# Values by tokens through DRAM, and base weights scaled by a norm, in a two-layer attention and FFN kernel

## The chip, the cores and the metric

The kernel runs on one core of one Trainium2 chip. The metric is the device time of one execution in microseconds (us), the median over runs. The core has TensorE for matmuls, VectorE and ScalarE, which read the matmul results in PSUM and work elementwise, GpSimd, which works elementwise on SBUF, and SyncE, whose queue issues every DMA of this kernel.

## What is computed

The input `x` and the context `ctx` are 32 batches of 128 x 1024, in f32. Two layers run one after the other on each batch; `LN` is a layer norm without weights.

```python
# layer 0, attention: autocorrelation of LN(x) with ctx, per head of 128 columns
corr = ifft(fft(q) * conj(fft(k))).real           # along the 128 rows
w, idx = top_k(corr, 9); w = softmax(w)
out += w[i] * v[min(idx[i] + pos, 127)]           # for the 9 best, v = ctx
x = x + out
# layer 0, FFN: base linear layer plus LoRA experts, the best 2 of 8
x = x + LN(x) @ W_base.T + b_base + lora(LN(x))
# layer 1, attention: 128 channels (rows), 1024 positions t (columns), 8 heads of 16 channels
q = Wq @ LN(x) + bq; k = Wk @ ctx + bk; v = Wv @ ctx + bv
k, v = pad(k, 8 left, 7 right, zeros), pad(v, same)
attn = softmax over the 16 positions t-8 .. t+7 of (q_t . k_j) / 4
x = x + Wo @ (attn . v) + bo
# layer 1, FFN: LoRA experts, the best 2 of 4
out = x + lora(LN(x))
```

## The kernel before

**Precision.** Most matrix products are made of f16 pieces: an operand is scaled, its high part is rounded to f16, and its low part is the remainder in f16. A product is then three f16 matmuls (high x high, high x low, low x high), accumulated in PSUM; the helper `three` and the table `THREE` stand for this. `split(hi, lo, src, eng)` makes the pieces: a ScalarE copy to the high part and a subtraction on VectorE or GpSimd (`G`). Some smaller products are done in f32 or in the matmul type f32r.

**Tiles.** `U()` is a 128 x 512 f32 buffer (tile u, 43 of them), `B()` a PSUM bank (p, all 8), `M()` 128 x 128 (m), `s()` small columns (s and t), and class `d` two buffers of 128 x 1024 f32. Any of them is given to an operation when the operation is placed, and comes free when its last user is done. Fixed tiles are, among others, `wsp` (the split base weights with the LoRA matrix and the router), `k16` (the split keys with 8 columns of zero padding on each side), `vpad` (the same for the values, high and low part side by side in one 4-byte word), `qbd` and `vbd` (block-diagonal stationary operands of the window attention).

**Stages of a batch**, by the names that the code gives to `P.stage`: `load` (ctx as `c`, x; ctx is scaled by its largest column maxima to the f16 pieces `c16`), `spec` (DFT of ctx; four copies inside SBUF move half of the partitions of each half batch), `corr`, `top` (the nine largest, on VectorE, and their softmax), `wt`, `inv`, then `ffn0`, `gate` and `base` for the first FFN, `kv`, `q`, `S` (scores), `PV`, `wo` for the second attention, and `ffn1`.

**The values.** In stage `kv`, `attention` computes V by channels: for each half of 512 positions, `three(p, wv16, c16[g])` gives 128 channels x 512 positions; ScalarE evicts it with scale and bias, and `split` writes both pieces to `vpad`. VectorE turns 32 x 32 blocks of `vpad`, seen as 4-byte words, through overlapping windows of 32 positions with a step of 16, into two tiles of class `d`, so that positions lie on partitions. For each half g and each group of 32 channels, an SP DMA then copies `d` to `vbd` in pieces of 128 bytes. `vbd` is one fixed tile: the loads of one half wait until PV of the half before is done. In stage PV, for each of 64 blocks of 16 positions, three matmuls of 32 columns take a 128 x 128 slice of `vbd` as weights and the split, transposed attention weights as the moving operand.

**The weights.** `prep_ffn` (stage `ws`) loads the base weights in 16 chunks of 128 x 512. VectorE takes the largest absolute value of each chunk per partition into `mx`, and likewise for the LoRA matrices; these are reduced over partitions with a transpose, and the results give the factors `wsc` (to the f16 range) and `wus` (back). Then the chunks are scaled and split into `wsp`.

**Order.** No engine's order is that of the code. A `Planner` records every operation with an estimated duration and then simulates the five engine queues in time; what it places on an engine, in which order, is emitted as written. Its priority for an operation is a period times the batch number, less the estimated length of the chain that follows, less a bias for the stage. `CFG` holds these numbers for two phases of time, with how many batches may be open at once (`win`: 5) and how many free buffers are kept back. After some batches the order repeats with a period.

All operations are recorded through one helper, so the profile gives nearly all of them the same line (L363); they are told apart by tile names and shapes.

Of the kernel before, what the change touches and what calls it, by code (L numbers as in the profile page):

```python
# [22 lines left out]
S = 128  # L23
# [5 lines left out]
CFG = {'nu': 43, 'nd': 2, 'en': 'G', 'cl': 'G', 'xl': 'G', 'sm': 'V', 'sw': 'A', 'wg': 'VG', 'q0': 'G', 'ns': 28, 'nt': 48, 'plan': {'phases': [{'at': 0.0, 'T': 19.88, 'margin': 178, 'win': 5, 'su': 60, 'sp': 3, 'ru': 1, 'rp': 0, 'bias': {'kv': -5.1, 'load': 10.0, 'S': -6.7, 'gate': 38.6, 'ffn1': 7.4, 'q': 0.4, 'top': 1.3, 'PV': -5.6, 'inv': 3.4, 'wt': 4.5, 'spec': 5.4, 'wo': 41.4, 'ws': -9.4, 'base': -1.7, 'ffn0': 90.1, 'corr': 5.4, 'setup': -12.6}}, {'at': 1459.1, 'T': 30.14, 'margin': 69, 'win': 6, 'su': 57, 'sp': 1, 'ru': 2, 'rp': 1, 'bias': {'kv': -32.9, 'load': -45.0, 'S': 18.4, 'gate': 125.0, 'ffn1': -67.8, 'q': 29.1, 'top': -23.6, 'PV': -37.2, 'inv': 57.1, 'wt': -20.7, 'spec': -56.0, 'wo': -29.3, 'ws': -71.2, 'base': -21.0, 'ffn0': 60.9, 'corr': -125.0, 'setup': 2.0}}], 'slack': [1.013, 0, 0]}}  # L29
# [11 lines left out]
class _View:  # L41
# [27 lines left out]
    def windows(self, n, step, width):  # L69
        return self._step("__getitem__", (slice(None), slice(0, 1)))._wrap(n, step, width)  # L70

    def _wrap(self, n, step, width):
        f = lambda ap: bass.AP(ap.tensor, ap.offset, [list(ap.ap[0]), [step, n], [1, width]])
        return _View(self.tile, f(self.proto), self.path + ((f, None, None),))

# [5 lines left out]

    def region(self):

        ap = self.proto
        size = mybir.dt.size(ap.dtype)
        dims = [list(d) for d in ap.ap]
        row = dims[0][0]
        p0, f0 = divmod(ap.offset, row)
        last = f0 + sum(s * (n - 1) for s, n in dims[1:])
        return p0, p0 + dims[0][1], f0 * size, (last + 1) * size  # L90


class _Tile:
    def __init__(self, cls, slot=None, const=False):
        self.cls, self.slot, self.const = cls, slot, const
        self.log, self.users = [], {}
# [9 lines left out]
class Planner:  # L106
# [72 lines left out]
    def _cost(self, op, method, v, kw):  # L179
# [21 lines left out]
        if eng == "Activation":  # L201
            op.dur += (n + (61 if src.proto.space == PSUM else 112)) / 1.2 + 94 * (nsc + ("accum_out" in v))
            if src.region()[0] != out.region()[0]:
                op.dur += 127.0
            elif out.proto.ap[-1][0] > 1:
                op.dur += 0.2 * n
        elif eng == "DVE":
            n = max(n, size(src))
            two = method in ("tensor_copy", "tensor_scalar", "memset") and not psum and n > 64
            op.dur += 6 * n / 0.96 + 67 if method == "reciprocal" else (n * (0.5 if two else 1.0) + 64 + 59 * nsc) / 0.96  # L210
            op.dur += 70.0 * ("accum_out" in v) + {"match_replace": 67.0, "transpose": 25.0}.get(method, 0.0)
        elif eng == "Pool":
            small = mybir.dt.size(out.proto.dtype) == 2
            if method == "memset":
                op.dur += 40.0 + (0.85 if small else 0.2) * n
            else:
                rate = (2.8 if small else 1.2) if method == "tensor_scalar" else 1.88 if small else 2.1
                if any(x.proto.ap[-1][0] == 0 for x in v.values()) and n > 128:
                    rate = 1.67
                op.dur += 530.0 if kw.get("op") == ALU.pow else 150.0 + rate * n  # L220
        else:
            run = out.proto.ap[-1][1] * mybir.dt.size(out.proto.dtype)
            dram = any(x.tile is None for x in v.values())
            op.dur += (3200.0 if dram else 2900.0 if run > 128 else 3500.0) + out.shape[0] * n * mybir.dt.size(out.proto.dtype) / 360.0

            op.cold = 450.0 if dram else 720.0 if run > 128 else 840.0

# [6 lines left out]
    def plan(self, phases, slack):  # L234
# [45 lines left out]
        while events:  # L280
            now = events[0][0]
            if phases and now >= phases[0][0]:
                period, window, margin, scarce, reserve, bias = phases.pop(0)[1]
                prio = lambda o: (period * max(o.batch, 0) - o.tail - bias.get(o.stage, 0.0), o.index)
                ready = {e: sorted((prio(o), o) for _, o in l) for e, l in ready.items()}
# [80 lines left out]
def plan_args(c):  # L366
    us = lambda v: v * 1e3
    scarce = lambda f: {"u": f["su"], "p": f["sp"], "d": 9, "m": 3, "r": 9, "s": 9, "t": 9}
# [6 lines left out]
def mk_kernel(ctx: ExitStack, tc: tile.TileContext, T: dict, out: bass.AP):  # L375
# [5 lines left out]
    pp = ctx.enter_context(tc.tile_pool(name="psum", bufs=1, space=PSUM))  # L381

    def slot(name, shape, dt=F32):
# [4 lines left out]
        "d": [slot(f"d{i}", [128, D]) for i in range(CFG["nd"])],  # L388
# [30 lines left out]

    def load(name, shape=None, dt=F32):  # L420
# [19 lines left out]
    G.memset(mhalf, -0.5)  # L440

# [20 lines left out]
    vpad = keep("vpad", [128, D + 16, 2], F16, 0.0)  # L462
# [21 lines left out]
    PE.matmul(pb[:, 0:3], lhsT=blk1, rhs=bsum, start=True, stop=True)  # L484
    bqs, sq, bqsc, uq = (const(n, [128, 1]) for n in ("bqs", "sq", "bqsc", "uq"))
# [6 lines left out]
    V.tensor_scalar(kvs[:, 1:2], rows[:, 2:3], C_SC / W_SC, None, op0=ALU.mult)  # L492
    V.tensor_scalar(kvb[:, 0:1], pb[:, 2:3], TINY, 1.0 / W_SC, op0=ALU.add, op1=ALU.mult)
    V.tensor_scalar(kvb[:, 1:2], absb[:, 2:3], TINY, 1.0 / W_SC, op0=ALU.add, op1=ALU.mult)
    V.tensor_scalar(rsx, rows[:, 1:3], 1.0 / W_SC, None, op0=ALU.mult)
# [25 lines left out]
    def prep_ffn():  # L521
# [10 lines left out]
        for k in range(16):  # L532
            t = U()
            SP.dma_start(out=t, in_=T["wbT"][k // 2 * 128 : (k // 2 + 1) * 128, k % 2 * HALF : (k % 2 + 1) * HALF])
            absmax(mx[:, k : k + 1], t)
            wb.append(t)
        for i in range(4):
# [7 lines left out]
        for i, (lo, hi) in enumerate(((0, 16), (16, 20), (20, 24), (24, 26), (26, 28))):  # L545
# [274 lines left out]
    def attention(b, x, c16, m1, sums):  # L820
        P.stage = "kv"

        bd, skv, bsc, esc, usc, eh = s(2), s(2), s(2), s(2), s(1), s(2)
# [3 lines left out]
        G.tensor_tensor(bsc, bkv_raw, skv, op=ALU.mult)  # L827
# [5 lines left out]
        for g in range(2):  # L833
            sl = slice(8 + g * HALF, 8 + (g + 1) * HALF)
            for i, (w, hi, lo) in enumerate(((wk16, k16[:, 0, sl], k16[:, 1, sl]), (wv16, vpad[:, sl, 0], vpad[:, sl, 1]))):
                t, p = U(), B()
                three(p, w, c16[g])
                A.activation(t, p, AF.Identity, bias=bsc[:, i : i + 1], scale=esc[:, i : i + 1])
                split(hi, lo, t, G)

        words = vpad.bitcast(U32).rearrange("p n i -> p (n i)")
        v16 = []
        for g in range(2):
            t = P.tile("d")
            tv = t.bitcast(U32).rearrange("p (b c) -> p b c", c=32)
            for h in range(2):
                V.transpose(tv[:, h * 16 : (h + 1) * 16], words[:, (2 * g + h) * 256 :].windows(16, 16, 32))
            v16.append(h16(t).rearrange("p (b c i) -> p b c i", b=32, i=2))
# [18 lines left out]
        for g in range(2):  # L867
# [4 lines left out]
            for hp in range(4):  # L872
                hs = slice(32 * hp, 32 * hp + 32)
                SP.dma_start(out=vbd[hs, :, hs], in_=v16[g][hs])
# [39 lines left out]
            V.scalar_tensor_tensor(x[g], p, bo, x[g], op0=ALU.add, op1=ALU.add, accum_out=sums[:, g : g + 1])  # L914
# [90 lines left out]
def _arrays(i):  # L1005
# [11 lines left out]
        "woT": a["L1_xattn_Wo"].T,  # L1017
# [22 lines left out]
```

## Time and profile before

| | |
|---|---|
| median of 3 runs | 1600.08 us (1599.47 to 1602.74) |
| profiled execution | 1600.9 us, its span 1599.1 us, mean granted TensorE clock 0.974 |
| TensorE busy | 1520.9 us, 95% of the span, 19144 matmuls |
| VectorE, ScalarE, GpSimd busy | 1468.7 us (92%), 1417.8 us (89%), 1346.0 us (84%) |
| DMA | 145.72 MB, queue busy 47.8% of 16 engines |
| first and last V matmul | 117.8 us, 1544.3 us |

A profile line of a group reads: engine, operation, output tile, input tiles, shapes, count, then busy time in us and the mean duration of one in ns, and the idle time just before these instructions with what ended it. Tile names stand without their numbers: u is any of the 128 x 512 buffers. A timeline line begins with start and length in us, and several equal instructions in a row are one line with a count. A line of the chain of waits begins with start and length in us. The granted clock is that of TensorE, as a share of full speed. The end of a matmul is modelled, so the pace of matmuls is read from starts.

### The profile page before, as it was taken

Reading aid. Unit: us, or ns where it says so; the run is one execution under the profiler, and the core shown is the slowest. Engines: PE = TensorE matmul, PEld = TensorE weight load, DVE = VectorE, ACT = ScalarE, POOL = GpSimd, SP = SyncE. Lnnn points to the kernel's source line nnn. Section 1 sums busy time; section 2 is a strip of 40 time slices with the busy share of each in tenths; the row PEclk is TensorE's granted clock in tenths of the full one; section 3 lists DMA queues with packets and bytes.
Section 4 is the critical chain, followed back from the end, with each engine's and each line's share of the span. In section 5 each row is a group of like instructions: output and inputs, shape, how many; then the busy total and the mean of one; then the engine's idle time right before and its main releaser. Section 6 shows DMA issues by size and latency. Waiting matters only on the chain.

```text
span 1599.1 us, 51794 instructions
## 1 busy us (share of the span) xinstructions
PE 1520.9 (95%) x19144; PEld 1001.9 (63%) x19144; DVE 1468.7 (92%) x5042; ACT 1417.8 (89%) x2833; POOL 1346.0 (84%) x1506
## 2 busy tenths in 40 slices
PE   2599999999999999999999999999999999999985
PEld 1256666666666666666666666666666666666654
DVE  6778999999999999999999999999999999999875
ACT  4998999999999999999999999999999999999753
POOL 5789878998888899888889988888998888899742
PEclk7789999999999999999999999999999999999996
DMA  8214544554454555445455544545455454554352
GB/s 267 81 56 57 98 63 91 102 105 91 91 91 70 94 102 106 91 91 92 69 96 101 105 91 92 93 68 96 100 105 92 90 95 68 95 100 78 41 70 58
DMA packets 854620, 145.72 MB, mean 91 GB/s; under 512 B 808224, under 2 KB 810528, under 8 KB 854368
## 3 DMA queue, kind: packets, MB, share of 16 engines
q1 hardware_dynamic: 854368, 142.41, 47.8%
q8 instruction: 152, 2.49, 0.7%
q14 instruction: 100, 0.82, 0.2%
HBM read 41.80 MB, written 16.78 MB: 37 GB/s over the span
## 4 chain that ended last, share of the span: by engine, by line
PE 90%; DVE 3%; ACT 2%; issue 1%; DMA 1%; POOL 1%; SPq 1%; POOLq 0%; DVEq 0%; ACTq 0%
PE p L363 90%; ACT u L363 2%; DVE u L363 1%; POOL u L363 1%; SPq L363 1%; DVE wsp L363 0%; DVE t L363 0%; DMA cf<-in_cf 0%; DVE s L363 0%; DMA u<-u 0%; DVE wmx L363 0%; DMA vbd<-d 0%; DVE mm L363 0%; DMA qbd<-u 0%; ACT k L363 0%
## 5 line engine op out<-in xcount | busy, mean ns | idle before, releaser
L363 POOL TENSOR_TENSOR u<-u,u 128x512 f32<-128x512 f32 (+1 forms) x640 | 774.9, 1233 | 94.4 <-ACT u L363 86.8
L363 PE MATMUL p<-wsp,u 128*128 128x512 f16 (+1 forms) x2304 | 409.9, 328 | 1.8 <-DVE r L363 0.9
L363 ACT ACTIVATE u<-p 64x512 f32<-64x512 f32 (+1 forms) x576 | 331.9, 591 | 52.0 <-PE p L363 43.7
L363 ACT ACTIVATE u<-u,t 128x512 f32<-128x512 f32 (+1 forms) x448 | 320.7, 723 | 62.3 <-DVE t L363 46.6
L363 DVE SCALAR_TENSOR_TENSOR u<-p,u 128x512 f32<-128x512 f32 (+1 forms) x448 | 289.2, 681 | 54.4 <-PE p L363 27.3
L363 PEld LDWEIGHTS <-u 128*128 128x128 f16 x3072 | 218.2, 98 | 167.0 <-issue 4.2
L363 ACT ACTIVATE u<-p,t 64x512 f32<-64x512 f32 (+3 forms) x448 | 265.7, 619 | 21.1 <-PE p L363 15.0
L363 PE MATMUL p<-u,ch 128*128 128x512 f16 x960 | 239.1, 385 | 1.9 <-DVE u L363 1.9
L363 PEld LDWEIGHTS <-qbd 128*128 128x128 f16 x6144 | 172.0, 96 | 27.1 <-issue 11.1
L363 PE MATMUL p<-k,qbd 128*128 128x32 f16 x6144 | 174.6, 176 | 1.6 <-issue 1.1
L363 PEld LDWEIGHTS <-ch 128*128 128x128 f16 x960 | 95.3, 102 | 120.7 <-issue 27.3
L363 PEld LDWEIGHTS <-vbd 128*128 128x128 f16 x6144 | 164.0, 97 | 8.5 <-issue 1.4
L363 PE MATMUL p<-u,vbd 128*128 128x32 f16 x6144 | 164.4, 176 | 0.7 <-POOL u L363 0.7
L363 ACT ACTIVATE u<-u,t,t 128x512 f32<-128x512 f32 x192 | 144.0, 820 | 5.2 <-POOL t L363 5.2
L363 POOL TENSOR_TENSOR t<-t,mhalf 128x1 f32<-128x1 f32 x128 | 71.5, 558 | 79.4 <-DVE t L363 79.0
L363 POOL TENSOR_TENSOR u<-u,s 128x512 f32<-128x512 f32 x128 | 134.2, 1050 | 0.7
L363 PE MATMUL p<-u,cf 128*128 128x512 f32 x256 | 125.2, 611 | 10.0 <-POOL u L363 10.0
L363 DVE SCALAR_TENSOR_TENSOR u<-p,t,u 128x512 f16<-128x512 f32 (+1 forms) x192 | 106.0, 567 | 16.9 <-ACT u L363 8.7
L363 ACT ACTIVATE u<-u 128x512 f16<-128x512 f32 x194 | 117.3, 623 | 3.4 <-DVE u L363 3.3
L363 PE MATMUL p<-ident,u 128*128 128x128 f32 x768 | 104.4, 279 | 10.6 <-ACT u L363 10.5
L363 PEld LDWEIGHTS p<-ident,u 128*128 128x128 f32 x768 | 90.8, 144 | 22.5 <-ACT u L363 13.4
L363 ACT ACTIVATE u<-p,t,t 128x512 f32<-128x512 f32 x128 | 94.0, 775 | 0.3 <-PE p L363 0.3
(155 smaller groups left out, 2863.8 us busy)
## 6 DMA issues: line engine op xcount, KB each, us to landing
vbd<-d SPq DMA_DIRECT2D x256, 128.0 KB
u<-u SPq DMA_DIRECT2D x192, 128.0 KB
u<-in_ctx SPq DMA_DIRECT2D x64, 256.0 KB
u<-in_x SPq DMA_DIRECT2D x64, 256.0 KB
qbd<-u SPq DMA_DIRECT2D x512, 32.0 KB
out<-u SPq DMA_DIRECT2D x64, 256.0 KB
u<-u SPq DMA_DIRECT2D x64, 126.0 KB
u<-in_wbT SPq DMA_DIRECT2D x16, 256.0 KB
```

The source lines that it names most:

```text
L363: fn(*[f(a) for a in args], **{k: f(a) for k, a in kw.items()})
```

## The change

**Values.** V is computed by tokens: for each block of 128 positions, the three pieces of the context are the weights (128 x 128) and `wv16` is the moving operand with 128 columns, so 12 matmuls of 128 columns fill one bank for each half. ScalarE evicts the high part to every second f16 place of a buffer, VectorE makes the low part from PSUM beside it, and an SP DMA writes the 512 positions (512 bytes each) to a DRAM tile, `vd[b % 2]`. The four `vbd` loads of each half read this DRAM tile in windows, in pieces of 128 bytes. `vpad`, class `d` and the VectorE transposes are gone.

As channels lie along the free dimension now, one scale serves all of them: the largest row sum and the largest bias over channels, made in setup (`gm`). The bias of V is not added to V: it goes through Wo into the output bias (`bo2`), and the padding rows hold the negative of the bias (`nbv`) instead of zero. Each batch writes these 2 x 8 padding rows by two small SP DMAs, after two ScalarE copies and a GpSimd subtraction on 16 partitions.

**Weights.** Instead of the 16 maxima on VectorE, ScalarE squares each chunk and sums the squares along the row (half a row of 1024); VectorE takes the largest of the 16 sums and GpSimd its square root.

**Plan.** `nu` goes from 43 to 49 u buffers, `nd` goes away. The numbers of `CFG` are others: the first phase has `win` 6, the second begins at 1494.3 in the planner's time instead of 1459.1, and each phase has biases for a stage on one engine too (`o.stage + "/" + o.eng`); estimated durations are stretched by 1.036 instead of 1.013, and DMAs get 0.27 us more. A DRAM tile counts as one region for dependencies.

```diff
-                prio = lambda o: (period * max(o.batch, 0) - o.tail - bias.get(o.stage, 0.0), o.index)
+                prio = lambda o: (period * max(o.batch, 0) - o.tail - bias.get(o.stage, 0.0) - bias.get(o.stage + "/" + o.eng, 0.0), o.index)
...
+    vd = []
+    for i in range(2):
+        vd.append(P.fixed(dp.tile([D + 16, 256], F16, tag=f"vd{i}", name=f"vd{i}")))
+        vd[i].tile.whole = True
...
+    mv, mx2, mb2, gm = const("mv", [128, 2]), s(1), M(), const("gm", [128, 2])
+    V.tensor_copy(mv[:, 0:1], rows[:, 2:3])
+    V.tensor_copy(mv[:, 1:2], absb[:, 2:3])
+    PE.transpose(pb[0:2, 128:256], mv, ident)
+    V.tensor_reduce(mx2[0:2], pb[0:2, 128:256], axis=AX.X, op=ALU.max)
+    V.tensor_copy(mb2[0:2], _bcast(mx2[0:2, 0], 128))
+    PE.matmul(pb[:, 256:258], lhsT=mb2[0:2], rhs=ident[0:2, 0:2], start=True, stop=True)
+    V.tensor_copy(gm, pb[:, 256:258])
+    bvr, nbv, bo2 = U(), const("nbv", [16, 128]), const("bo2", [128, 1])
+    SP.dma_start(out=bvr[0:16, 0:128], in_=T["bvr"].broadcast_to([16, 128]))
+    V.tensor_scalar(nbv, bvr[0:16, 0:128], -1.0, None, op0=ALU.mult)
+    PE.matmul(pb[:, 264:265], lhsT=woT, rhs=bkv_raw[:, 1:2], start=True, stop=True)
+    V.tensor_scalar(bo2, pb[:, 264:265], bo, None, op0=ALU.add)
...
-            absmax(mx[:, k : k + 1], t)
+            A.activation(U(), t, AF.Square, accum_out=mx[:, k : k + 1])
             wb.append(t)
+        V.tensor_reduce(mx[:, 30:31], mx[:, 0:16], axis=AX.X, op=ALU.max)
+        V.tensor_scalar(mx[:, 31:32], mx[:, 30:31], TINY, None, op0=ALU.add)
+        G.tensor_tensor(mx[:, 0:1], mx[:, 31:32], half, op=ALU.pow)
...
-            for i, (w, hi, lo) in enumerate(((wk16, k16[:, 0, sl], k16[:, 1, sl]), (wv16, vpad[:, sl, 0], vpad[:, sl, 1]))):
-                t, p = U(), B()
-                three(p, w, c16[g])
-                A.activation(t, p, AF.Identity, bias=bsc[:, i : i + 1], scale=esc[:, i : i + 1])
-                split(hi, lo, t, G)
-        words = vpad.bitcast(U32).rearrange("p n i -> p (n i)")
-        v16 = []
-        for g in range(2):
-            t = P.tile("d")
-            tv = t.bitcast(U32).rearrange("p (b c) -> p b c", c=32)
-            for h in range(2):
-                V.transpose(tv[:, h * 16 : (h + 1) * 16], words[:, (2 * g + h) * 256 :].windows(16, 16, 32))
-            v16.append(h16(t).rearrange("p (b c i) -> p b c i", b=32, i=2))
+            t, p = U(), B()
+            three(p, wk16, c16[g])
+            A.activation(t, p, AF.Identity, bias=bsc, scale=esc[:, 0:1])
+            split(k16[:, 0, sl], k16[:, 1, sl], t, G)
+        vb = vd[b % 2]
+        t, u = M(), M()
+        pads = h16(u).rearrange("p (n r) -> p n r", r=2)
+        A.activation(t[0:16], nbv, AF.Copy, scale=skv[0:16, 1:2])
+        A.activation(pads[0:16, :, 0], nbv, AF.Copy, scale=skv[0:16, 1:2])
+        G.tensor_tensor(pads[0:16, :, 1], t[0:16], pads[0:16, :, 0], op=ALU.subtract)
+        for i in range(2):
+            SP.dma_start(out=vb[i * (D + 8) : i * (D + 8) + 8], in_=h16(u)[8 * i : 8 * i + 8])
+        for g in range(2):
+            t, p = h16(U()), B()
+            with P.group():
+                for n in range(4):
+                    for i, (m, r) in enumerate(THREE):
+                        PE.matmul(p[:, n * 128 : (n + 1) * 128], lhsT=c16[g][:, m, n * 128 : (n + 1) * 128],
+                                  rhs=wv16[:, r], start=i == 0, stop=i == 2)
+            v = t.rearrange("p (n r) -> p n r", r=2)
+            A.activation(v[:, :, 0], p, AF.Copy, scale=esc[:, 1:2])
+            V.scalar_tensor_tensor(v[:, :, 1], p, esc[:, 1:2], v[:, :, 0], op0=ALU.mult, op1=ALU.subtract)
+            SP.dma_start(out=vb[8 + g * HALF : 8 + (g + 1) * HALF].rearrange("(n p) e -> p n e", p=128),
+                         in_=t.rearrange("p (n e) -> p n e", n=4))
...
-                SP.dma_start(out=vbd[hs, :, hs], in_=v16[g][hs])
+                SP.dma_start(out=vbd[hs, :, hs].rearrange("p b n r -> p b (n r)"),
+                             in_=vb.grid(g * HALF * 256 + 64 * hp, ((256, 32), (16 * 256, 32), (1, 64))))
...
-            V.scalar_tensor_tensor(x[g], p, bo, x[g], op0=ALU.add, op1=ALU.add, accum_out=sums[:, g : g + 1])
+            V.scalar_tensor_tensor(x[g], p, bo2, x[g], op0=ALU.add, op1=ALU.add, accum_out=sums[:, g : g + 1])
```

## The prediction, made before the changed kernel had run

> **What bounds the kernel now.** I read the page's engine table and slices first, then the granted windows, the chain of waits in order of time, the groups by shape, and last the timeline of TensorE and ScalarE.
>
> ```profile
> PE 1520.9 (95%) x19144; PEld 1001.9 (63%) x19144; DVE 1468.7 (92%) x5042; ACT 1417.8 (89%) x2833; POOL 1346.0 (84%) x1506
> PE   2599999999999999999999999999999999999985
> ```
>
> TensorE is the busiest engine, and its idle time sits in the first two slices and the last two. The windows cut the span there (columns: busy us of each engine, granted clock, DMA share, GB/s):
>
> ```profile
> 0.00:100.00 100.00, 49.73 (x189) 28.28 (x190) 75.81 (x279) 71.87 (x139) 67.83 (x81) 0.74 0.48 148
> 100.00:217.00 117.00, 113.48 (x1282) 72.24 (x1281) 102.10 (x343) 106.08 (x208) 106.31 (x113) 1.00 0.44 76
> 217.00:1508.00 1291.00, 1290.97 (x16566) 853.55 (x16566) 1231.70 (x4266) 1195.45 (x2404) 1136.19 (x1271) 1.00 0.50 90
> 1508.00:1600.00 92.00, 66.69 (x1111) 47.86 (x1109) 59.09 (x155) 44.39 (x87) 35.62 (x44) 0.82 0.40 64
> ```
>
> From 217 to 1508 us TensorE never stops, at full clock; 50.3 us of its idle lie before 100, 3.5 between 100 and 217, 24.4 behind 1508 (the span ends at 1599.1). The chain of waits says the same, and what ends last outside the long stretch:
>
> ```profile
> 22.27 6.07 DMA u<-u
> 30.35 2.96 DVE wmx L363 x5
> 33.38 2.01 DVE wmx L363 x10
> 36.93 0.79 DVE mm L363 x4
> ...
> 217.03 1290.31 PE p L363 x16561
> 1508.05 2.73 DMA vbd<-d
> ```
>
> A second such wait of 2.71 us stands at 1554.5. So three stages have three limits: a start led by VectorE (chain 28 to 57 us) and then by all elementwise engines, a long stretch that only TensorE's own work can move, and a serial tail.
>
> **TensorE's part.** Now V takes six 512-column matmuls a batch; after, 24 of 128 columns, each with its own weights. Paces are read from starts:
>
> ```profile
> 742.95 0.92 PE L363 MATMUL p<-ar,u 128*128 128x68 f16 x24
> 743.71 1.46 PE L363 MATMUL p<-wsp,u 128*128 128x512 f16 x6
> 745.00 2.75 PE L363 MATMUL p<-u,ch 128*128 128x512 f16 x12
> ...
> 1509.93 0.87 PE L363 MATMUL p<-wsp,u 128*128 128x136 f16 x12
> 1510.64 0.60 PE L363 MATMUL p<-ident,u 128*128 128x128 f32 x4
> ```
>
> 24 of 68 columns with a weight load each take 0.76 us (31.7 ns), six of 512 take 1.29 (215 ns), 12 of 136 take 0.71 (59.2 ns). The line through 68 and 136 gives 56 ns at 128 columns. So 24 x 56 = 1.34 us against 6 x 215 = 1.29: +0.05 a batch, +1.7 over 32. At 59.2 ns each it would be 1.42, +4.2; the low end is 55.7 ns (59.2 x 128/136), +1.5. I take +1.7.
>
> Here a rule speaks against the change. The Trainium skill (TensorE: Matmul & The Clock Gate, "Back-to-back issue gap") gives about 81 ns for each 128-column matmul in a stream that also loads weights. By it the sum would be an estimated 24 x 81 = 1.94 us a batch, +20 us in all, and the change would be slower. The 136-column row of this trace, wider and also one weight load per matmul, runs at 59.2, so I keep the row.
>
> **The elementwise part of V,** per batch, by these rows:
>
> ```profile
> L363 DVE STREAM_TRANSPOSE d<-vpad 128x512 uint32<-128x512 uint32 x128 | 88.2, 691 | 0.6 <-POOL vpad L363 0.5
> L363 POOL TENSOR_TENSOR vpad<-u,vpad 128x512 f16<-128x512 f32 x64 | 81.7, 1279 | 2.7 <-ACT vpad L363 2.7
> L363 ACT ACTIVATE vpad<-u 128x512 f16<-128x512 f32 x64 | 46.4, 811 | 0.0
> L363 DVE TENSOR_REDUCE wmx<-u 128x1 f32<-128x512 f32 x16 | 9.8, 672 | 0.0
> ```
>
> VectorE loses 4 x 0.691 = 2.76 us and gains two PSUM steps to f16 (the like of it, from p and t into u, has a mean of 744 ns): 1.49; net -1.28. GpSimd loses 2 x 1.279 and gains one 16 x 128 subtraction, at most 0.42 (on the line between 128x36, 244 ns, and 128x512 f16, 1163 ns): -2.1. ScalarE loses two evictions (775 ns) and two strided copies (811), 3.17; it gains two evictions to strided f16 (686 for the unstrided one, plus the 192 by which vpad's copy exceeds k16's 619: 0.88 each) and two pad copies of at most 0.40 (128x128 with a scale, 402 ns): 2.56; net -0.6. None of it counts in the long stretch, where TensorE is what lies on top at 1290.97 of 1291 us. In the start it can count only behind 117.8 us, the first V matmul, where TensorE's idle is at most the 3.5 us above; I take -1.5, bounds 0 and -3.5.
>
> **The detour through DRAM.** A batch gains four issues (two writes of 256 KB, two pad writes) on SP's queue, and the eight vbd loads read DRAM in pieces of 128 B instead of SBUF. SP is not near full: its issues between 690 and 736 us add up to about 29 us of 46.6, and four more at the 0.43 to 0.69 us of present ones are 1.7 to 2.8. What waits on SP: the writes for VectorE's low part, the loads for the writes' landing; behind them queue the next qbd loads and input loads. V has room: its matmuls end at 679, the loads of the first half are issued at 698.1, and PV reads them at 714.8. A write of 256 KB at the 2.7 us that the first ctx load took (0.72 to 3.38) is landed before 690. The tight place is the second half's load: issued 671.4 to 674.6, read at 681.8, so 7.2 us from last issue to use, of which 2.7 are needed now (chain rows). No row here reads 128 B pieces from DRAM; the bounds are 2.7 and the 6.07 us of the u<-u transfer caught in the weight loads. Both fit in 7.2, so this costs nothing in the long stretch.
>
> The Trainium skill (DMA: Bandwidth & Descriptors, "Why small descriptors are slow (HBM only)") says that small pieces are penalised with HBM on one side and not from SBUF to SBUF, which is the step made here. It gives no landing time for this shape, and no row here shows one.
>
> **The weight scale.** Sixteen maxima of 0.672 leave VectorE (10.75 us). Of these, ten were done between 15 and 22 us, ahead of VectorE's 6.4 us wait for the u<-u transfer, and gain nothing; six lie at 29.1 to 33.3 on the chain, 0.26 + 2.96 = 3.2 us of it. Behind them the first top-k (mm, 36.9) waited, though its correlation was done on TensorE at 33.5. So -3.2; bounds 0 (something else queued there) and -3.4 (33.5 to 36.9). In their place ScalarE gets 16 squares with accumulation:
>
> ```profile
> 109.72 0.71 ACT L363 ACTIVATE u<-u,t 128x512 f32<-128x512 f32 x1
> 110.34 0.19 ACT L363 ACTIVATION_READ_ACCUMULATOR u<-u,t 128x1 f32 x1
> ```
>
> The next one starts at 110.43: 0.71 each, 11.4 us. The cover is ScalarE's idle time from 24.4 to 31.1, 31.3 to 35.3 and 36.8 to 39.8, 13.8 us, with the last weight chunk issued at 19.8. If that cover is gone the 11.4 stand in 40 to 100 us, where ScalarE is busy 55.7 of 60. The scale itself (a power on GpSimd, 0.56, and two small steps) comes some 3 us later than now; what hides that is that the weights it scales are first read by TensorE at 88 us, 47 after the scale. Setup gains about ten VectorE steps of 0.14 to 0.27, 1.6 us, for the common V scale and the folded bias; VectorE is 19.1 of 20 busy at 40 to 60, and I charge half: +0.8, bounds 0 and 1.6.
>
> **Order and buffers.** Six more u buffers, two DRAM images in place of one vpad, and a new order for every engine. No row prices a plan. What the tail shows is two waits for vbd loads, 2.73 and 2.71 us; an image per parity lets V be ready earlier, a load still has to land. I take half, -2.7, between 0 and -5.4. Reordering may cost as much as it gives elsewhere in the 24.4 us of idle tail: +-5 in the range.
>
> **Sum** against the profiled execution (1600.9 us, 1.8 of it outside the span; 0.8 above the median): +1.7 - 1.5 - 3.2 + 0.8 - 2.7 = -4.9, so 1596.0, and by the median 1595.2. I say 1595. All low ends at once give -10.8 (1.5 - 3.5 - 3.4 - 5.4), all high ones +5.8 (4.2 + 1.6), the reordering aside; they hardly come together, so this case's own range is 1587 to 1599.
>
> **Rivals.**
> - *Nothing reaches the end.* VectorE's freed start is filled by the next elementwise work and the tail keeps its waits: 1600.1 + 1.7 + 0.8, less half of the start's 4.7: about 1600. For it: from 40 to 100 us VectorE, ScalarE and GpSimd are 74 to 93% busy. Against: the top-k waited for VectorE alone.
> - *Slower: the squares stand in the way.* ScalarE runs in order. If its squares are placed ahead of evictions, or behind 40 us, the start lengthens by their 11.4 us where ScalarE leads the chain (64 to 69 and 84 to 88 us): 1600.1 + 11.4 + 1.7 + 0.8, with only the 1.5 and 2.7 kept as gains: 1609.8. It decides once more than about 5 us of squares lie outside the idle times named above, which pays for the other gains.
> - *The detour is late.* A load that needs over 7.2 us stops TensorE once a batch; at 0.5 us late over the 28 batches of the long stretch, 14 on top of the forecast: 1609. Against: 6.07 was the slowest seen here.
>
> **How the numbers follow.** The forecast 0.58, nothing 0.14, squares 0.20, detour 0.08. About 0.2% (3.2 us) is what a measurement of this kernel can tell from no change; nearly all of the first case clears 1596.9, a little does not, and a part of "nothing" falls on each side: faster 0.56, same 0.15, slower 0.29. The range 1584 to 1609 goes from all low ends with 5 us of luck in the order to the near part of the slower cases.
>
> **What would show it.** Right: unbroken TensorE from before 214 us, a period of 46.6 us between PV groups, 128-column V matmuls 56 ns apart, no wmx on VectorE's chain before the first top-k, squares ended by 36 us, no TensorE wait for vbd. Wrong: TensorE idle between 217 and 1500, V matmuls at 80 ns, squares between evictions behind 40 us, or a tail longer than 92 us.

## The result and the profile after

The changed kernel takes 1617.13 us (median of 5 runs, 1613.55 to 1618.67) against 1600.08 us (1597.83 to 1602.74) of the kernel before: 1.0101 times, interval 1.0085 to 1.0118. The forecast was 1595 us, from 1584 to 1609. The profiled execution took 1617.13 us, its span 1615.3. These are the lines of the page and of the windows that answer to those of before:

```profile
PE 1532.2 (95%) x19725; PEld 1031.4 (64%) x19725; DVE 1437.4 (89%) x4972; ACT 1420.6 (88%) x2865; POOL 1287.4 (80%) x1475
HBM read 75.36 MB, written 33.82 MB: 68 GB/s over the span
```

```profile
0.00:100.00 100.00, 49.49 (x199) 27.51 (x200) 68.92 (x271) 79.94 (x169) 68.89 (x84) 0.78 0.55 167
100.00:217.00 117.00, 114.69 (x1251) 73.66 (x1250) 99.98 (x341) 108.45 (x215) 101.93 (x111) 0.99 0.46 70
217.00:1508.00 1291.00, 1284.31 (x16889) 870.10 (x16887) 1196.05 (x4169) 1175.01 (x2373) 1068.84 (x1226) 1.00 0.58 101
```

TensorE is no longer unbroken between 217 and 1508 us, though VectorE and GpSimd have less to do there. The first product with `wk` of each batch dates the batches in the timeline. For batch 3 and batch 28, two lines of before (L363) and two of after (L364):

```profile
252.14 1.46 PE L363 MATMUL p<-u,wk 128*128 128x512 f16 x6
1417.14 1.46 PE L363 MATMUL p<-u,wk 128*128 128x512 f16 x6
253.20 0.81 PE L364 MATMUL p<-u,wk 128*128 128x512 f16 x3
1434.02 1.24 PE L364 MATMUL p<-u,wk 128*128 128x512 f16 x5
```

From batch 28 to the end of the span it is 182.0 and 181.3 us. So in these two profiles the start lost 1.1 us, the tail gained 0.7, and the long stretch lost 15.8 in 25 batches. The first two are within what one profile can tell: four runs below that leave the start as it is have batch 3 at 251.5 to 253.2, and two that leave the tail as it is take 181.1 and 182.0 for it. Before, each batch of the stretch takes 46.60 us to the digit; after, 47.05, and some batches up to 1 us more: 25 x 0.45 = 11.2, and 4.6 of single stops.

The chain of waits shows the 0.45. Where it had one line for the stretch, it now leaves TensorE once a batch:

```profile
784.04 39.65 PE p L364 x550
823.69 0.02 issue
823.71 0.61 ACT u L364
824.32 0.02 issue
824.34 1.29 DVE u L364 x2
...
828.55 0.33 ACT p L364
...
829.61 0.63 ACT u L364
830.24 0.03 issue
830.27 0.79 ACT u L364
831.05 0.04 issue
831.10 1.02 PE p L364 x4
```

TensorE's matmul at 831.10 waited for ScalarE's instruction at 830.27. ScalarE's timeline names it:

```profile
827.04 0.77 ACT L364 ACTIVATE u<-p,t,t 128x512 f32<-128x512 f32 x1
827.84 0.68 ACT L364 ACTIVATE u<-p,t 64x512 f32<-64x512 f32 x1
828.55 0.33 ACT L364 ACTIVATE p<-p,t,wus 128x8 f32<-128x8 f32 x1
828.90 0.68 ACT L364 ACTIVATE u<-p,t 64x512 f32<-64x512 f32 x1
829.61 0.63 ACT L364 ACTIVATE u<-u 128x512 f16<-128x512 f32 x1
830.27 0.78 ACT L364 ACTIVATE u<-p,t,t 128x512 f32<-128x512 f32 x1
```

The lines at 827.04 and 830.27 evict the two halves of K. The second stands in ScalarE's queue behind the gates' exponential (wus), which waits for a chain of VectorE steps. The base matmuls need its bank: their step from 830.60 takes 495 ns, not 216.

The single stops lie elsewhere, in the S matmuls. TensorE's timeline around one:

```profile
595.46 2.56 PE L364 MATMUL p<-u,vbd 128*128 128x32 f16 x96
597.86 0.38 PE L364 MATMUL p<-band_b,ident_b 128*128 128x512 bf16 x1
598.08 1.36 PE L364 MATMUL p<-k,qbd 128*128 128x32 f16 x48
599.29 0.38 PE L364 MATMUL p<-band_b,ident_b 128*128 128x512 bf16 x1
599.50 0.45 PE L364 MATMUL p<-k,qbd 128*128 128x32 f16 x12
600.78 0.87 PE L364 MATMUL p<-k,qbd 128*128 128x32 f16 x28 [0.83 <-issue]
```

There are ten such stops, 5.3 us together, all where the new order puts the S pair (two runs of 48 score matmuls, each behind one `band_b` product) straight behind a PV pair (96 matmuls): 194 matmuls and as many weight loads in 5.2 us. "Issue" means that nothing in the profile was waited for. The page lists 156 transfers of instructions of 16 KB, 0.9 to 1.7 us each; for TensorE's 39450 matmuls and weight loads that is one for about 250, so they are taken for TensorE's:

```profile
q8 instruction: 156, 2.56, 0.7%
```

Each stop ended some 1.3 to 1.6 us after the end of such a transfer that had fallen into the dense run. Eight other dense runs of the stretch had one too, ended 1.9 us or more before the run did, and did not stop, so a transfer there is not enough by itself. Before, a base step lies between PV and S, and no S run stops.

### The profile page after: what moved, and what is told of

Its sections match the earlier page's. It is cut to its first block, busy times and chain, and to the rows that moved or that the text cites. A ratio compares the mean times of both kernels' runs of the same rounds, so it can differ in the third digit from the quotient of the medians.

```text
span 1615.3 us, 52919 instructions
## 1 busy us (share of the span) xinstructions
PE 1532.2 (95%) x19725; PEld 1031.4 (64%) x19725; DVE 1437.4 (89%) x4972; ACT 1420.6 (88%) x2865; POOL 1287.4 (80%) x1475
## 4 chain that ended last, share of the span: by engine, by line
PE 80%; DVE 9%; ACT 7%; DMA 1%; issue 1%; POOL 1%; SPq 0%; POOLq 0%; ACTq 0%; DVEq 0%
PE p L364 80%; ACT u L364 6%; DVE u L364 6%; DVE mm L364 1%; ACT p L364 1%; DVE s L364 1%; POOL u L364 1%; DVE t L364 0%; DVE wsp L364 0%; DMA u<-in_ctx 0%; DMA u<-u 0%; DMA u<-in_bvr 0%; DMA u<-in_x 0%; DVE m L364 0%; POOL wsp L364 0%
## 5 line engine op out<-in xcount | busy, mean ns | idle before, releaser
L364 POOL TENSOR_TENSOR u<-u,u 128x512 f32<-128x512 f32 (+1 forms) x640 | 772.0, 1235 | 179.2 <-ACT u L364 163.2
L364 PEld LDWEIGHTS <-u 128*128 128x128 f16 x3840 | 274.5, 98 | 227.7 <-issue 46.8
L364 PE MATMUL p<-wsp,u 128*128 128x512 f16 (+1 forms) x2304 | 403.9, 328 | 5.3 <-DVE u L364 1.7
L364 ACT ACTIVATE u<-p 64x512 f32<-64x512 f32 (+1 forms) x576 | 332.3, 593 | 51.8 <-PE p L364 44.6
L364 ACT ACTIVATE u<-u,t 128x512 f32<-128x512 f32 (+1 forms) x448 | 306.8, 712 | 54.5 <-DVE t L364 43.0
L364 ACT ACTIVATE u<-p,t 64x512 f32<-64x512 f32 (+3 forms) x512 | 316.4, 650 | 36.1 <-DVE t L364 17.8
L364 DVE SCALAR_TENSOR_TENSOR u<-p,u 128x512 f32<-128x512 f32 (+1 forms) x448 | 294.3, 683 | 41.6 <-ACT u L364 34.9
L364 PE MATMUL p<-u,ch 128*128 128x512 f16 x960 | 243.5, 385 | 4.1 <-POOL u L364 2.4
L364 PEld LDWEIGHTS <-qbd 128*128 128x128 f16 x6144 | 171.1, 96 | 24.5 <-issue 5.0
L364 PE MATMUL p<-k,qbd 128*128 128x32 f16 x6144 | 176.1, 176 | 3.8 <-issue 3.7
L364 PEld LDWEIGHTS <-vbd 128*128 128x128 f16 x6144 | 167.9, 97 | 14.6 <-issue 10.6
L364 PE MATMUL p<-u,vbd 128*128 128x32 f16 x6144 | 169.5, 177 | 6.2 <-ACT u L364 3.6
L364 DVE SCALAR_TENSOR_TENSOR u<-p,t,u 128x256 f32<-128x256 f32 (+1 forms) x256 | 150.1, 618 | 18.0 <-ACT u L364 15.8
L364 PEld LDWEIGHTS <-ch 128*128 128x128 f16 x960 | 89.9, 99 | 112.3 <-issue 43.6
L364 ACT ACTIVATE u<-u,t,t 128x512 f32<-128x512 f32 x192 | 146.8, 815 | 11.1 <-POOL u L364 5.0
L364 ACT ACTIVATE u<-u 128x512 f16<-128x512 f32 (+1 forms) x210 | 129.3, 636 | 12.7 <-DVE u L364 9.6
L364 POOL TENSOR_TENSOR u<-u,s 128x512 f32<-128x512 f32 x128 | 133.2, 1051 | 0.8
L364 PE MATMUL p<-u,cf 128*128 128x512 f32 x256 | 130.1, 611 | 2.6 <-POOL u L364 2.6
L364 PEld LDWEIGHTS p<-ident,u 128*128 128x128 f32 x768 | 91.5, 143 | 47.9 <-ACT u L364 18.2
L364 PE MATMUL p<-ident,u 128*128 128x128 f32 x768 | 104.8, 278 | 16.4 <-ACT u L364 9.0
L364 POOL TENSOR_TENSOR t<-t,mhalf 128x1 f32<-128x1 f32 x128 | 72.2, 564 | 51.5 <-DVE t L364 50.8
L364 DVE TENSOR_REDUCE s<-p 128x16 f32<-128x512 f32 x128 | 87.6, 685 | 15.6 <-PE p L364 15.5
```

The source lines that it names most:

```text
L364: fn(*[f(a) for a in args], **{k: f(a) for k, a in kw.items()})
```

## The theories

- **A, the order:** the loss comes from the new order of the instructions, not from what they do.
- **B, the detour:** V's way through DRAM (75 MB read, not 42) or the work it adds makes TensorE wait.
- **C, the squares:** ScalarE's squares hold the start back and eat the gain there.

Most runs below keep the changed kernel's recorded work and change only the list that the planner made, after it was made. `ahead(o, z)` puts instruction o just in front of z in `P.order`, where nothing between them touches o's operands or buffers.

## Experiments: the detour

**No detour, same order.** The writes of V are not issued and `vbd` is loaded from a constant.

```diff
             SP.dma_start(out=vbd[hs, :, hs].rearrange("p b n r -> p b (n r)"), ...)
+            P.ops[-1].calls[-1][2]["in_"] = dftk[hs, 0, 0:64].unsqueeze(1).broadcast_to([32, 32, 64])
```

> The changed kernel with its order of instructions kept, but V's way through DRAM taken out: the four writes of V per batch are not issued, and the loads of vbd read 128 B pieces of a constant tile in SBUF, so its output is not the attention's. If the loss of 17 us comes from the order (theory A), the base matmul's wait of 0.28 us per batch and the period of 47.05 us stay, and the time is 1612 to 1617 us. If it comes from the detour, its transfers or the DRAM reads (theory B), the period returns to about 46.6 us and the time is 1599 to 1604 us.

Measured: 1616.67 us, 1.0095 times before (1.0079 to 1.0110). The traffic is that of before again, and nothing else moved:

```profile
HBM read 41.81 MB, written 16.78 MB: 36 GB/s over the span
```

The period is 47.05 us, the waits for K's bank add up to 6.9 us, and eight stops in S to 4.8. So the way through DRAM costs nothing here. This run keeps the work that the change adds on ScalarE and VectorE, the other half of B; the mended order below answers that half.

## Experiments: the order of the stretch

**K's eviction early.**

```diff
+    first, second = [o for o in evicts if o.batch == b]          # b from 4 to 27
+    ahead(second, P.order[P.order.index(first) + 1])
```

> The changed kernel, in which ScalarE evicts the second half of K right behind the first, ahead of the gates' exponential, in batches 4 to 27; all else is in the same order. Theory A: TensorE's wait of 0.28 us in the base matmuls, once a batch, is for the bank that this eviction frees, so it goes in 24 batches: -6.7 us, 1610 us, unless the gates' chain is now late, which would show as a wait at the gates' transpose. Theory B: the wait comes from the extra work on the engines, moves elsewhere, and the time stays at 1616 to 1618 us.

Measured: 1610.29 us, 1.0058 (1.0043 to 1.0073). The period is 46.78 us, and the chain of waits of this run has one line for the window in which it had 24:

```profile
783.99 48.18 PE p L364 x636
```

The queue place of one ScalarE instruction was worth 0.27 us a batch, 7 us. The stops in S stayed (ten, 6.0 us).

**A base step between PV and S.**

```diff
+        if prev.stage == "PV" and o.stage == "S" and o.batch < 30:
+            ahead(next(z for z in te[te.index(o):] if z.stage == "base"), o)
```

> The changed kernel, in which TensorE does one base step (6 matmuls, 1.3 us) between a PV pair and the S pair that followed it at once; all else is in the same order. In the changed kernel ten S runs stop for 0.2 to 0.98 us, 5.3 us in all, and each stop ends 1.3 to 1.6 us after the end of a transfer of TensorE's instructions. Theory A (the order packs 388 short instructions into 5.2 us, and they run out): the ten stops go, -5 us, 1612 us. Theory B (S waits for its operands, which the new traffic makes late): the stops stay or move, 1616 to 1618 us.

Measured: 1621.67 us, 1.0127 (1.0110 to 1.0144), slower. All ten stops went, every batch now takes 47.42 us; but the move made S and `wo` 1.3 us later, and VectorE, which runs in order, stood for the projection:

```profile
794.44 0.75 DVE L364 SCALAR_TENSOR_TENSOR u<-p,bo,u 128x512 f32<-128x512 f32 x1 [1.25 <-PE p L364]
```

What is queued behind it on VectorE then made TensorE's transposes wait 0.2 us a batch, more than half of the 0.37 that the period grew. The cure was right and its place wrong.

**The projection and a base step between the two S runs,** so that the first S run is not later.

```diff
+            for stage in ("wo", "base"):
+                ahead(next(z for z in te[i:] if z.stage == stage), te[i + 1])
```

> The changed kernel, in which TensorE does the projection (wo) and one base step between the two S runs that follow a PV pair, so the first S run starts when it did; batches 4 to 28. The dense stretch is 290 short instructions, not 388. Theory A (the order): the wait of the first trial, in which everything from S on came 1.3 us later and VectorE stood 1.25 us before the projection's sum, does not come, because the first S run and the projection are not later; most of the ten stops in S (5.3 us) go: 1612 to 1614 us. Theory B (S waits for its operands): the stops stay, 1616 to 1618 us.

Measured: 1613.37 us, 1.0073 (1.0058 to 1.0088); six stops are left, 2.75 us.

**Both, and two moves in the start** (those of the next section).

> The changed kernel with four moves together: K's second eviction ahead of the gates' exponential, the projection and a base step between the S runs, eight squares early, the bias loaded early. If each gives what it gives alone and none makes the next wait: 7 us for K's eviction, 4 us for S, 2 to 6 us in the start, so 1600 to 1605 us, level with the kernel before; if the order has no slack left (each cure makes another chain late), 1608 to 1612 us.

Measured: 1615.85 us, 1.0086 (1.0071 to 1.0101). The parts did not add up: with K evicted first, ScalarE's eviction of PV comes some 0.3 us later, and `wo`, which needs VectorE's step behind it, starts 0.17 us later in 21 batches (period 46.94 us). Batch 3 took 49.94 us: a stop of 1.28 us in S was followed by half the clock, as in the run with the bias early (last section). And the moves in the start are no gain by themselves, as the next section shows.

**The two that count, base step first.**

```diff
-            for stage in ("wo", "base"):
+            for stage in ("base", "wo"):
```

> The changed kernel with the two moves of the stretch that each gave time, K's second eviction ahead of the gates' exponential and work between the two S runs, with the base step ahead of the projection (with the projection first and both moves, TensorE stood 0.3 us for ScalarE's eviction of PV, which the moved K eviction pushes back). Theory A: the two add up, the period is 46.78 us with few stops, and the time is 1605 to 1608 us, still above the kernel before by the f32 entries and V's pace (some 4 us) and by the start. If the order has no slack, a third wait appears and the time stays at 1610 to 1614 us.

Measured: 1605.42 us, 1.0028 (1.0019 to 1.0037). 12 of the 17 us are back. The period is 46.69 us: 0.09 less, because `wo` (f32) no longer follows S directly. In the traces of these runs an f32 product right behind short f16 ones takes some 0.08 us more for its first step, called an f32 entry below: `wo` 512 ns behind S, 429 ns behind a base step.

**Two f32 entries less.** The product with `ones` goes behind the PV pair, one product with `bl` ahead of the router's short ones.

```diff
+        if o.stage == "load" and te[i - 1].stage == te[i + 1].stage == "PV":
+            ahead(te[i + 1], o)
+        if o.stage == "base" and len(o.calls) == 3 and te[i - 1].stage == te[i + 1].stage == "ffn1":
+            ahead(o, te[i - 1])
```

> The two moves of before (1605.4 us) and the two f32 entries, without the halved base step. Theory A: the period goes from 46.69 to 46.53 us, under the 46.6 us of the kernel before, and some eight stops in S stay: 1600 to 1603 us. If the entries are only a way of counting, the period stays at 46.69 us and the time at 1605 us.

Measured: 1603.66 us, 1.0013 (1.0004 to 1.0022). The period is 46.60 us; of two entries, one was saved. Seven stops (4.8 us) stayed.

**The base step in halves** (three matmuls ahead of the first S run, three and `wo` ahead of the second), with the moves above.

```diff
+            step.calls, rest.calls, rest.allocs = step.calls[:3], step.calls[3:], []
+            ahead(step, o)
+            ahead(rest, te[i + 1])
```

> The changed kernel, with its order mended in four places: K's second eviction early; half a base step ahead of the first S run, the other half and the projection ahead of the second (from batch 2 on), so that no dense run is longer than 192 short instructions; the sum over the context's maxima (ones) behind the PV pair, not inside it, and one f32 product (bl) ahead of the short router products, not between them, which saves two f32 entries of 0.08 us per batch. Theory A: against the two moves alone (1605.4 us) the last eight stops go (4.4 us) and two entries per batch (4.5 us): 1596 to 1600 us, at or under the kernel before. If half a base step ahead of the first S run makes VectorE late, as in the first trial, the period rises over 46.7 us and the time is 1606 to 1612 us.

Measured: 1601.76 us, 1.0002 (0.9993 to 1.0011): level with the kernel before. The stretch is as it was before the change, 46.60 us in nearly every batch, and no S run stops for more than 0.1 us. So the 0.45 us is 0.27 for K's bank and 0.18 for the neighbours of f32 products, and the rest was stops; with one f32 entry saved, the change's own work takes no longer than the old, and the second half of B falls.

**The planner's numbers.** Two runs give the old numbers to new work, so each has an order that nobody chose.

```diff
-CFG = {'nu': 49, ... numbers of the kernel after}
+CFG = {'nu': 49, ... numbers of the kernel before}
```

> The code of the changed kernel, planned with the numbers of the kernel before (biases, windows, no biases by engine), so that the planner makes another order of the same work. Theory A (the order sets the loss): the time moves by several us against 1617 us, in either direction, and where the base matmuls' wait and the stops in S are missing the stretch runs at 46.7 to 46.8 us per batch. Theory B (the work added by the change sets it): 1615 to 1619 us again, with a stretch of 47.0 us.

> The kernel before with V by tokens through DRAM alone: maxima on VectorE as before, the planner's numbers of before, the buffers of after (49 wide ones). The planner makes a new order of its own from it. Theory A: the time follows the order, and V through DRAM costs TensorE no more than the slower pace (+1.2 us) and a few f32 entries: 1594 to 1606 us. Theory B: the stretch runs at 47 us per batch again, 1614 to 1620 us.

Measured: 1626.53 us, 1.0162 (1.0147 to 1.0177), for the changed code; 1612.41 us, 1.0072 (1.0057 to 1.0087), for V by tokens alone, where three batches take 140.2 us, 46.75 each, without stops in S. The first is as A says, 9 us from the changed kernel by the order alone; the second lies between the two theories, with 0.15 us more per batch than before and the rest lost outside the steady batches. Here numbers found for one piece of code did not carry over to another.

## Experiments: the start

**Squares alone,** maxima replaced in the kernel before, with its numbers.

> The kernel before with the base weights' scale from squares on ScalarE alone, V as before, planned with the numbers of the kernel before. Theory C (squares behind ScalarE's queue hold the start back): the stretch runs at 46.6 us per batch, but it begins later, and the time is 1603 to 1610 us. If the squares are hidden, 1597 to 1600 us. Theory A adds that the new order can by itself move the stretch either way; then its period is not 46.6 us.

Measured: 1651.28 us, 1.0311 (1.0294 to 1.0329). Beyond all that was expected, and no answer to C: the batches are 5 to 94 us apart, so the planner's order broke down as a whole.

**No squares, order of the changed kernel.**

```diff
             A.activation(U(), t, AF.Square, accum_out=mx[:, k : k + 1])
+            P.ops[-1].calls.clear()
```

> The changed kernel in its order, but the sixteen squares are not issued and the base weights' scale is a constant, which leaves that scale out of the computation. Theory C (the squares, 11 us on ScalarE, hold the start back): batch 3's K product starts 3 to 6 us earlier than 253 us, and the time is 1611 to 1614 us. If VectorE and the loads end the start in any case, batch 3 starts at 252 to 254 us and the time stays at 1615 to 1618 us; the squares then cost nothing, and the maxima they replaced gave nothing either.

Measured: 1613.99 us, 1.0082 (1.0066 to 1.0097); batch 3 at 248.3 us, not 253.2, nor 251.5 as in the earliest of the runs with the same start. C holds: in this order the squares cost the start some 3 to 5 us, of which 3.1 show in the time. ScalarE's timeline in the changed kernel shows why:

```profile
22.46 2.54 ACT L364 ACTIVATE u<-p,t 64x512 f32<-64x512 f32 x4
30.04 0.81 ACT L364 ACTIVATE u<-u,t,t 128x512 f32<-128x512 f32 x1 [5.04 <-POOL u L364]
31.28 0.63 ACT L364 ACTIVATE u<-u 128x512 f32<-128x512 f32 x1 [0.42 <-DVE wmx L364]
...
50.70 0.62 ACT L364 ACTIVATE u<-u 128x512 f32<-128x512 f32 x1
...
55.22 2.13 ACT L364 ACTIVATE wsp<-u,wsc 128x512 f16<-128x512 f32 x4 [2.36 <-DVE wsc L364]
```

The first square (31.28) is queued behind an instruction that waits 5 us for GpSimd; the last is at 50.70, and the weights are first scaled at 55.22 (without squares at 51.5). TensorE, in the changed kernel, then stands for the scaled weights, which it does not without squares:

```profile
88.98 4.34 PE L364 MATMUL p<-wsp,u 128*128 128x136 f16 x23 [0.58 <-DVE wsp L364]
```

**Eight squares earlier, and the bias earlier.**

```diff
+    for o in squares[2:10]:
+        ahead(o, gap)
```

> The changed kernel, in which eight of the sixteen squares go on ScalarE ahead of batch 1's normalisation, which waits 5 us for GpSimd there, and write their unused result over a part of wsp that is filled later; all else is in the same order. Theory C (the squares in ScalarE's queue hold the scale wsc back, and the start with it): wsc is ready some 5 us earlier than at 55 us, and the gates' first matmuls and the end come 2 to 5 us earlier, 1612 to 1615 us. Rival: another chain (the transfers, VectorE) ends the start anyway, and the time stays at 1617 us.

> The changed kernel, in which the small load of V's bias (bvr) is issued ahead of the sixteen loads of base weights, not behind them, into a tile of its own. In the changed kernel VectorE's nbv stands 4.3 us for it on the chain of the start. If that wait counts, the end comes 2 to 4 us earlier, 1613 to 1615 us; if the squares behind it hold the start in any case, it stays at 1617 us.

Measured: 1621.58 us, 1.0132 (1.0115 to 1.0148), and 1619.19 us, 1.0107 (1.0091 to 1.0123). The first did not do what it said. `gap` was the second normalisation, so the squares went behind the waiting instruction and in front of the top-k's evictions; the scale came 1.7 us later. All its squares also wrote one unused buffer, which put them 0.75 us apart and not 0.61, some 2 us over sixteen; how much of the delay is the place and how much the buffer is not shown. The second took the load out of VectorE's way, but nbv still began at 33.26 us and the scale came only 0.4 us earlier. The chain of waits misleads here: it gives the load 4.31 us up to its landing, while VectorE itself had other work and stood 0.28 us:

```profile
28.71 4.31 DMA u<-in_bvr
```

```profile
33.04 0.50 DVE L364 TENSOR_SCALAR nbv<-u 16x128 f32<-16x128 f32 x1 [0.28 <-DMA u<-in_bvr]
```

**Squares into ScalarE's gaps, on the mended order:** eight ahead of the waiting instruction, each with an unused result of its own; then the same with the bias early; then six more in other gaps.

```diff
+        junk = wsp[:, 1, k // 2, k % 2 * HALF : (k % 2 + 1) * HALF]
+        o.calls[0] = (o.calls[0][0], (junk,) + o.calls[0][1][1:], o.calls[0][2])
+        ahead(o, first if k < 8 else second if k < 10 else evict if k < 11 else top)   # k from 0 to 13
```

> The kernel with the mended order (1601.8 us), and eight of the sixteen squares now truly ahead of the instruction that waits 5 us for GpSimd on ScalarE (the first trial had put them behind it), each with an unused result of its own in wsp. Without any squares the scale wsc was ready at 51.3 us, not 55.0, and the kernel ended 3 us earlier. Theory C: eight squares (4.9 us) go into the idle 25 to 30 us, wsc comes at 51.5 to 53 us, and the time is 1597 to 1600 us, under both kernels. If the weights have not landed by 25 us, or another chain ends the start, the time stays at 1601 to 1603 us.

> The same with the small load of V's bias issued ahead of the base weights' loads, so that VectorE's nbv does not wait until 33 us. By itself that moved wsc by 0.4 us only, because the squares stood behind it; with the squares out of the way the wait may count: 1595 to 1599 us. If the next thing on the chain (a spectrum's transfer that lands behind the weights) ends at the same time, no difference from the run beside it.

> The kernel with the mended order, and fourteen of the sixteen squares put into ScalarE's idle stretches of the run before: eight ahead of the wait for GpSimd (25 to 30 us), two ahead of the second normalisation, one ahead of a spectrum's eviction, three ahead of the top-k's exponentials (36 to 38 us); two stay where they were. Theory C: wsc comes some 3.5 us earlier than in the run with eight moved (its first use at 53.5 us), near the 51.5 us of the run without squares, batch 3 starts at 248 to 250 us, and the time is 1597 to 1599 us, under the kernel before by 0.15% or more. If the start is now ended by VectorE or by the transfers, 1600 to 1601 us.

Measured: 1600.46 us, 0.9997 (0.9988 to 1.0006); with the bias 1601.04 us, 1.0002 (0.9993 to 1.0010), no difference. With fourteen moved, 1598.21 us, 0.9979 (0.9970 to 0.9988): faster than both kernels. ScalarE's timeline and the window of the stretch in that run:

```profile
22.52 2.54 ACT L365 ACTIVATE u<-p,t 64x512 f32<-64x512 f32 x4
24.95 0.62 ACT L365 ACTIVATE wsp<-u 128x512 f16<-128x512 f32 x1
...
29.24 0.62 ACT L365 ACTIVATE wsp<-u 128x512 f16<-128x512 f32 x1
...
51.49 2.13 ACT L365 ACTIVATE wsp<-u,wsc 128x512 f16<-128x512 f32 x4 [2.36 <-DVE wsc L365]
```

```profile
217.00:1508.00 1291.00, 1290.12 (x17064) 879.04 (x17061) 1201.20 (x4193) 1186.36 (x2393) 1081.60 (x1239) 1.00 0.58 102
```

The weights are scaled from 51.49 us on, as without squares, batch 3 starts at 249.5 us (before: 252.1), and TensorE is at 1290.12 of 1291 us again. All of the change is in this kernel; only its order differs, and where unused squares go. The kernel before had no such mending by hand, so what it would gain from one stays open.

## Why the prediction was wrong

- **Order and buffers, the step that failed.** It was priced in the tail alone, -2.7 and +-5, because the prediction read the long stretch as one "that only TensorE's own work can move". That was true of the old order, whose banks came free in time. It was carried over to an order that had not been seen. The stretch lost 15.8 us by it: 11.2 by K's bank and f32 neighbours, 4.6 by stops. The unbroken 1290 us was read as slack on the other engines. It was not ScalarE's load that broke it, 1175 us of 1291 with the loss and 1186 in the last run above without it, but one instruction's place in its queue. In the tail both waits for `vbd` left the chain (one is left, 0.2 us), but other chains end there: it gained 0.7 us in these profiles, no more than two profiles differ by, not 2.7.
- **The weight scale.** The freed chain came as read: the first top-k began at 33.85 us, not 36.85. The cover did not. The idle time from 24.4 us was counted as room for 6.7 us of squares without asking what stood ahead of them in ScalarE's queue. Four of the sixteen were done by 38 us, and the scale came at 55.0 us, where the forecast had it some 3 us behind the old 41.2. The 47 us between the scale and its first use on TensorE did not hide that: the weights are scaled one after another until 94 us, and TensorE came to wait for them. The forecast's -3.9 for the whole start (-1.5, -3.2 and +0.8) became +1.1. The rival "squares stand in the way" had this mechanism (5 us outside the gaps) but only this part of the loss.
- **TensorE's part held.** Twelve V matmuls take 0.67 us (816.65 to 817.32 in the line below), 56 ns each. The Trainium skill's 81 ns (TensorE: Matmul & The Clock Gate, "Back-to-back issue gap") would have cost 25 ns more on each of 768, and the trace does not show it.

```profile
816.65 0.83 PE L364 MATMUL p<-wv,u 128*128 128x128 f16 x12
817.32 1.35 PE L364 MATMUL p<-u,vbd 128*128 128x32 f16 x48
```

- **The detour held** at nothing, by the first experiment. Pieces of 128 B took 15.9 ns of a DMA engine in the changed kernel against 12.3 before; in the first experiment, where they come from SBUF, it was still 15.4, so DRAM is not shown to be what slows them. The slack of 7.2 us covered it.
- **The setup** missed the bias load behind 4 MB of weights; it cost 0.28 us on VectorE, within the 0.8 charged.
- **The sum** came near what the changed kernel gives once its order is mended, -4.9 forecast and about -3.3 measured (0.21% of 1601.4), but in part by luck. In that run's profile the start gains 2.6 us, the stretch loses 0.9 and the tail 0.2; and the mended order also saves an f32 entry (0.09 us a batch, some 2 us), while the kernel before was not mended.

## What to carry to other kernels

An engine that never idles shows that the present order feeds it, not that only its own work can move it; where a change brings a new order, price the steady period too, by who frees each PSUM bank and what is queued ahead of that instruction. Idle time on an in-order engine is cover only for work placed ahead of the instruction that waits. When a tuned order comes with new code, compare the period of the steady batches first, and undo the order, not only the code, before the code is blamed.

## What the hardware showed unexpectedly

- TensorE can stop where nothing in the profile holds it. In runs of about 390 short instructions it did in 10 of some 28 batches; with no run longer than 98 matmuls and as many weight loads, none to two times in the five runs so ordered. That the transfers of instructions cause it fits the times of the stops, but not the eight runs with a transfer and no stop, and no run acted on these transfers alone: the cause is not shown.
- A stop can cost more than its length. In the run with the bias early, a stop of 1.28 us in S at 267.4 us was followed by a window at a lower granted clock, in which six base matmuls took twice their time; batch 3 took 49.94 us, nearly 3 us more than the steady ones. The run with all four moves has the same stop and the same drop in batch 3. Two lines of the run with the bias early, and one of the run with K's eviction early, behind a stop of 1.36 us at 923.8 us:

```profile
267.20:268.70 1.50, 0.22 (x10) 0.14 (x6) 1.50 (x3) 1.50 (x4) 0.00 (x0) 1.00 0.72 207
268.70:272.80 4.10, 4.10 (x27) 1.71 (x27) 1.78 (x7) 0.66 (x2) 2.46 (x3) 0.58 0.20 23
...
925.20:929.30 4.10, 4.10 (x68) 2.63 (x69) 2.89 (x6) 2.07 (x4) 2.41 (x3) 1.00 0.36 82
```

  The Trainium skill (TensorE: Matmul & The Clock Gate, "Part 1: The HAM clock gate (the "warmup" mystery)") puts the drop behind an idle window of about 3.4 us. Here stops of 1.28 us, next to many 32-column matmuls, were followed by it in two runs; stops of 1.36 us, next to the same matmuls, in two others (the one shown and the run with two f32 entries less), and those of up to 0.98 us in the changed kernel, were not. So the length of the stop alone does not decide, and what does is open.
- Squares that write the same unused buffer one after another are 0.75 us apart, with buffers of their own 0.61.
